# First attention of a two-layer block on one Trainium2 core: running sums by a scan with channels on partitions, in place of triangle products with tokens on partitions

## The chip, the cores and the metric

One core of a Trainium2 chip runs the whole program. The metric is the device time of one execution in microseconds (us); the time of the kernel is the median of ten runs. Engine names are those of the profile: PE is TensorE (matmul), PEld its weight load, DVE is VectorE, ACT is ScalarE, POOL is GpSimd, SP is SyncE, which here only issues transfers.

## The reference, cut to what matters

The input is 16 sequences of 512 tokens with 128 channels. Four stages follow each other, each with a residual and a layernorm: a first attention (below), a mixture of 8 experts that sends every token to one expert, a second attention (softmax, 16 heads of 8 channels, with a bias by distance), and a second mixture with a shared expert. Only the first attention changes. It is a linear attention with 16 heads of 64 value channels; `cexp` is the exponential of a clipped argument:

```python
cross = einsum('bnw,hw->bhn', x, k1) + p1         # p1, p2: sums of sines of the position
diag  = einsum('bnw,hw->bhn', x, k2)
extra = einsum('bnw,hw->bhn', x, k3)
values = einsum('bnw,hwa->bhna', x, value_weight)
cross, diag, extra, p2e = cexp(cross), cexp(diag), cexp(extra), cexp(p2)
num = cumsum(cross * values, axis=2) * p2e * extra + values * diag
den = cumsum(cross, axis=2) * p2e * extra + diag
out = einsum('bhna,hwa->bnw', num / den, output_weight)
```

So for each sequence, head and value channel there is a running sum over 512 tokens, and each token and head has three gates (`cross`, `extra * p2e / den`, `diag / den`) that hold for all 64 channels of the head.

## The kernel before, in words

The 16 sequences go through the four stages in six chunks of 2, 3, 4, 3, 3 and 1. The second attention of a chunk runs together with the first attention and the first mixture of the next chunk and with the second mixture of the chunk itself. Every piece of work is an `op` with an engine, a planned cost, and the buffers that it reads and writes. The order of all ops is written out as a string of two-character ranks (`ORDER`, line 54), and a chain of dependencies without semaphores keeps each engine's instructions in that order. So an instruction that waits holds all that stands behind it on its engine, and SP's transfers too are issued in the order of the list.

Buffers come from pools with fixed counts: `pair` (two PSUM banks, 128 x 1024 f32, three of them), `one` (one PSUM bank, two), `wide` (128 x 1024 f32 in SBUF, twelve), `row` (128 x 512 f32 in SBUF, eleven).

`attention0` makes the gates of one sequence with tokens on partitions: `sc` holds the three scores of each token and head, `ex` their exponentials, `ce` the running sum of `cross` (by products with the triangle `tri` and with ones, L966 and L968), and `den`, `gg` (that is `extra * p2e / den`) and `own` (`diag / (cross * den)`) follow in small VectorE steps (L976 to L990).

`tile0` then does the value part for one sequence and one tile of 128 tokens, four tiles in a row, all 16 x 64 channels side by side in the free dimension:

- PE makes `pv`, the values (L1015, two products of 512 columns); DVE multiplies by `cross` into `ev` (L1028).
- POOL makes `self`, the token's own term, from `ev` and `own` (L1034).
- For tiles 1 to 3 a transfer issued by POOL adds the last row of the tile before (`carry`) to the first row of `ev` (L1041).
- PE makes the running sum `cum` by a product of `ev` with the triangle `tri` (L1050); ACT copies its last rows to `carry` (L1057) for the next tile.
- DVE multiplies `cum` by `gg` into `o` (L1062) and adds `self` (L1066).
- PE turns `o` in eight 128 x 128 transposes into `po` (L1073), ACT copies it to `ot` (L1076), PE multiplies `ot` with the output weights into `y` (L1081), and DVE adds `y` to the tile of `x` (L1089).

So a sequence passes four tiles, each with five `wide` buffers and three `pair` buffers, and each waiting on the carry of the one before.

The rest of the kernel is not touched. Of it, the text names: the second attention's bias add `p<-st,bias` (DVE, L1441) with the exponential (ACT, L1447), its row maxima `low` (bf16, ACT L1333, DVE L1349, L1365 and L1376), its inputs `qk_pad`, which SP loads (L1272, L1285, L1405); and the fetches of expert weights and token rows by indirect transfers that POOL issues (L796).

Of the kernel before, what the change touches and what calls it, by code (L numbers as in the profile page):

```python
# [19 lines left out]
P = 128  # L20
# [34 lines left out]
    "#$###)#9#-#0#.#&#%#(#A#D#'#,#B#G#J#=#7#H#I#K#*#?#L#M#O#F#P#Q#R#W#X#Y#6#C#T#U#Z#<#>#S#a#d#@#3#[#i"  # L55
    "#k#N#4#^#f#m#`#g#l#n#o#t#{#}#/#2#1$-#s#x$4$2$/$c#_#5#r&:#+#:#;%H'Y#u#8#v#w#V#]#b#~$#$$#c#p$'$&$+"
    "$)$*$0$3$:$A#e#z$,$.$7$9$8$<$B$E$K$]$1$6$;$?$D$H$L$M$N$[$a$e$C$G$I$J$T$U$W$Y$b$h$u$y%'%J%Q%R%W%["
    "%l#E#|$F$O$P$S$V$Z$Q$R$f$X$^$`$g$j$k$q%5$_$d$i$m$n$o$v$w$x${%*%@$l$p$r$s$|%,%)%+%-%2%E%M$z%$%(%."
    "%/%6%8%<%A%B%K%N%S%X%Y%^%`%b%c%d%e%f%m&8&Q&q'2&9&?&>&G&H&I&U&Y'.&E&o&R&Z&t&{&}&~'5'$'&'%'3'>'@'P"
    "'['e'#']'T'V'h'n't'u'v(/(2(4(=(@(d(r(s*>+T#y#h#j#q$%$($5$=$t%w$>%1&7%v'A'f(I(G%y'*&i%x$@$}%z'B(>"  # L60
    ")5'?-.(K%t(B(C(S(W(D(O(T(P(N(Y)>)&)d)=(U(x(q(V([)T)e)S)g)<)J)K({(~)$)Q)*)+)-(l(z(})E)1)6)9)C)G)I"
    ")X)m)3):)@)/)2)4)H)r)u*)*;*L)')F(e(k)?)f)c*P*Z*T*U*f*_*w*})O)V)^)Y)Z)j)v*|*`*c*{+'+-+9)W)])i)7)8"
    ")D)x*o*n*t++*u+/+A)N)P)U)(),)0*,*3*z+#+(+>*~+8+K*(***0*#*$*'*5*6*7*S*[+&+N+Q+Y)a)b)R)`+*+5+I+4+G"
    "+H+L+_+P+[+k*:*=*@)s)t)y*A+@+R+X+a+D+W+p*<*B*E)w)z)|*F+E+`+d+s+F+Z+}*C*D*I*4*8*9*J*K+6+g+l+x+;+C"
    ",*)p)~*&*+*/*1*p*q*r*x*y+J,0,4,<*.*-*G*%+h,/,&+n,,+b+f+o,1,8,9*M*Y*^*g*h*i+0+r+w+z,2+v+{,:*]*a*b"
    "*d*e*l+=+i+|,#,@+m+y,C*k*m*s+$+%+.+2+B,%,),5,E,',3,P+1+:+?+)+7+<+O+U+c+t,$,(,X,],`,W,A,F,S,Z,b,m"
    ",N,O,U,d,R,g,w,l,Q,T,[,n,p,~,^,_,i,v,a,j-+-1-5-=-E-[-_-t-u.).8.J.K.u.}.W.r.[.`.x/5/;1H,+,-,e,f,."
    ",7,=,>,D,B,;,M,?,r,H,K,V,L,J-8,s-9-W-/-4-<-2-3-;-O,u,{,}-'-)-0-K-?-A-C,|-#-*-Q-X-&-(-,,h,o,x-R-Y"
    "-Z.$.%.+,I,z,y,q-I---:-V.A.@.I.L.D.Y.c-L-P-`-6-@-B-m.M.S.U.a.O.X.p-d-f-h-J-M-]-p.Q.d.g.s.V.b.~-G"
    "-S-^-e-i-l-n-o.k.h.m.n.t.y/E-a-c-g-s-x-y-z.0.3.B.G.^/F/O/b-U-T-k-H/R.q/V/T/#/I/J/_/'/B/f.,.-.5-v"  # L70
    "-}-~/,/?/K/Q/^/G/H/p.>.E.H./.=.?.j/M/`/g/r/W/d/{.w.z.{.v.|/%/-/./o/h/k/s/v/}/~.e.f.i.6.7.9.l///0"
    "/@/D/j0#0005._.C-{.Z0$0%0+0,/y/w/x0;0)0K0O/$/&/)/*/+/1/<070*0/0J090I0U/(/2/6/[/a/e/i/z030?0Z0.0E"
    "0]/4/8/=/7/>/C/P/U0A0H0P0_0G0Q0b/L/N/]/X/c/q0'0(060=0F0L0q0u0z0W0M0S0T0X0`0k0N0R0V0a0^0h0l0[0i0r"
    "0t0m0o0|0d0n0y1%0v1'1(1)1,1.1415181@1A1C1N1Q1R1^1a1]1b1`1d1g2s3-:{$~%#%%%&%0%4%7%9%3%:%;%?%I%C%D"
    "%F%O%a%i%=%>%L%P%V%_%Z%]%o%{%|&.%T%U%g%h%j&$%n%u&&&'&)&+%p%q%s&%&*&/&2&3&6&=&S'8'F'Z(.(1(8(H%k%r"
    "%G%}%~&#&,&1&;&(&-&A&0&5&<&B&C&F&j&k&4&@&J&K&L&N&V&W&[&c&d&p&D&M&O&P&a&f&g&h&l&r'1'7&`&e&s&w&x&y"
    "&z'+'4':'G'H'L'i'}(#(g(m&X&T&]&^&_&b&u&v&m&n&|'''-'(')'6'9'M'N','/'='D'E'O'J'K'Q'S'a'k';'<'I'R'W"
    "'X'_'`'g'y'z($'U'^'p'q'w'x'|'~()(+(,(-(E(X(f(h(n(u(w(|)%).)[)k*?+~/:/A*R*j*v+,+M+V+e+j-7*Q+q+]+^"
# [12 lines left out]
    "6k6q797%9m9.9l928V8m8o8|8W8d9+7B7M7O767?7@7d8l8t8y9$8x9)9@7]7f7g7I7N7R7k9#8}9'9,909L9d7n7w7z7p7|"
    "8*8.8?8w9?9A9^8~9D9g7U7W7Z7V7Y7[7l8A979O9W9y9p9v9w7J7t7K7<9n9q9o9_:&9z:$:,:':.:K8E8J8M7^7b7i8N:9"
    "9~:#:1:@:C:L9F9K9M9E9J9S9T:-:(:5:6:7:;:M9(93959&9/999;9=:D:):4:=:Q:R:e9V9f9h9Q9R9Y9{:/:<:A:B:N;+"
    ";3;O:U:O:V:i:`:h:~:d:W:b:c:s;#;):r;(;*;1:y;0;@:a;,;2;<:g;5;A;H;K;W;k;l;x;y;{<<<=<D<L<O<Y<s=$<w<|"
    "='=2=HC/:*:0:^:k:8:H:::>:G:S:Y:j:E;n:X:o:]:l:m:x<,:n<%;G;J;Q;%;&;-;];7;>;?;6;;;C;[;P;R;U;V;Z;^;d"
    ";e;.;:;=;j;r;v;};~<#<F<G<H:z:|:p:q;D<Q<P=:<r<b<c=(<v=*=8;S;`;b;X;_;c;w<u=0=5==<z=)=F;z<'</;E;I;M"
    "<2=,=6=;=O=.=Q=r;h;p<$<?<A<K<S<W=1=>=C=P=4=<=z<&<)<3<0<1<5<l<m<q<t<y=7>$>'>.;m;t<+<-=c>>=N=y=n=Z"
    "=_=o=u=}>*<e<j<o<f<h<i=U=G=s=v>(=X=p>E<U<X<[<N<V<a<k={=w=|>:=~>;>H<><B<R<~=%=&=V=W=e>3>8>9=q>1>L"
    "<*<6<7<8<@<E<}=Y=h=t=x><>M>Y>d<^<`=/<]>f>j>l>g>@>A>Q>R>I>W>h=K=S=`=E=J=L>&>B>O>a>v>F>G>}=3=@=A=d"
    "=g=l>)>i>]>`>z>s?#?$=i=j=m=[=b=f>+>C>N>e>r?%>[>b?+>#>0>7>,>->6>K>P>S>Z>c>p?3?4?9>t>y>{?/>w?,?1>x"  # L100
    "?(?*?<>|?5?J?&?.?:?@?-?;?K?)?2?7?I?6?B?L?N?P?R?S?T?U?V?W?X?_?`?a?b?c?j?y?n?s?}@)@bK4'0'C'b'c'd'j"
    "'l'm'o'r's'{(((%('(5(6(9(:(&(*(0(3(<(L(?(A(R(](i)#(7(;(M(Q(a(p(b(c(j(t)h)}(Z(`);)B)L)M)l+S+u-r-|"
    ".'.4.F.N.T.].o5#(J(F(^(_(o)))A)n(v(y){)_)q)o*2*H*O*V*X,c,t->-N.#.&.(.R0&0-0B0j*N*W.1.20Y0f0c0e0s"
    "0}1?1E0:0@0g0w1/11121;1K1V1_1n1p2*2[2n3?3C-j-$040<0p1$1*191&1-1I1M1U1Y1Z1e1t3`3r1>1S1W1X2&2-2+28"
    "494=5W5f2%2)273)5/5=5I5O5h5i6H6I4O4U5B5C5]5m5o5r5v6Q6y7;8)888<8K8Q8T412{4~565[5g5j5w5n5q6@6-6466"
    "6S6T6W757H6V6Y6a6e7P7X7Q7c7j7x828F6[6d7/7e848>8D8Z8^8i8r8z8'838@8P8[8b8h8q8s9%9*9-919B9C9G9H9I9P"
    "9Z9[9]9c:t:u:w9k;8=?:};9;T;a;u<(<9<:<_;o<C<.<4<n<p<x<{>n<I=-=#=+=B=D=R=]>o<J=a=^=k>%>2>4>D>m=M>^"
    ">J>T>_>k>q>u?D>=?'>~?0?8?=?A?F?G?H?Y?]?g?k@-@5@RB'C%@4DRD|GFG{B*DNH~J4KK?d?m?t@.?e?f@L@o?i@p@dAt"
    "A~AuB8B=BKB[BWBfBrC+C-C6BXC5CACVC`D'CbCcD(D<DBHfDxE5F-F0GPGcGSGUGeGvH%K5EiHDGmGyHmI,HuH}I0JgJtKq"
    "FnMGJQJ[MgN%MjMkN*N2N<N@NrO9O>OWOcPNQAP+P,QmVbX4ZVbqR1RKS;UbVAVDYV>X?l?o?~@&?p?z?w?q?u?|@$@A@F@Z"  # L110
    "?{@H@C@@@B@DAr@EA)@c@e@m@_@`@f@{@r@s@xA+A,A0A4@g@h@n@k@q@t@|A&@vA#A$@~A%A'A5A:A<AcAdAv@,@+@>@=@G"
    "A(A2A;AxAwAyB4B#B,B?@;@J@K@S@T@Y@]B3A|B(BCB:BIBR?O@1@3@M@O@P@QB>B2B6BBBFBSBU@'@0@8@9@I@N@y@zBDB;"
    "BABGBQBVB^@7@:@?@U@W@[@aA1A3AQAhA}BaBdBwAIA=AHA/BvBNBeBOBMB+B5BbBPBYBqB%B&B-B)B/B0B7BZBlBmBnB]Bi"
    "ByAzA{B$AXA_AaB.B_BoBpBsBjBkC1AbAfAkA]A`AeB9BHB}B|C&C(C)C2C3AiAjAnApAqAsB1BLBTB`BcBzC7C;CKA-A.@l"
    "@jC#C>B~CSC=C0C:CJC@CICOA6A7A8@u@w@}A9C,C?CDCNC4CLCPAJAKANALAOASAYC.CFCQCgC9CMCxACAFAMA@AAADAUAV"
    "CHCTC_C|CWCzD.APARATABAEAGAZA[A^BEBJC$D@DMDoD-CvC}D#D3D7DGCXCyC~D5CYCiDLDJC{D%D1DPDYD[D0D4D;DID:"
    "DCD_DfDjE%E(E2E9E?EFEMEYEdE{F:FMF;FQF<F?FUG1G6L5C[C]E,E=CaCdCfChCeCjCnCwD]D/CoD6CtD*CsDVDtDgD~D8"
    "D?DDDQDXDaE&DODUDZDTDWDeDvDcDmDnD^DbDlE'E+D=DEDKD>DADSDwE-E.ECEEEPD`D9DHD2EADdF(D{E]E`ElEzE^EfF'"
    "E:E>E@D}E*E/EWF.F+F2F6F3F8FAE1E4E8E$E0E6EJEhF1F=FCEnEsFHEBEHEIE3E7E;E[EpF7FNFSFWF>FaFbEGEKELDkDp"
# [156 lines left out]
def block_kernel(ctx: ExitStack, tc: tile.TileContext, d, out: bass.AP):  # L276
# [16 lines left out]
        "st": (sm, [P, NT, 6], F32, 2),  # L293
        "mv": (sm, [P, NT, 2], F32, 2),
        "rs": (sm, [P, 2, NT], F32, 2),
        "ex": (sm, [P, NT, 3 * H0], F32, 2),
        "gg": (sm, [P, NT, H0], F32, 2),
        "den": (sm, [P, NT, H0], F32, 2),
        "own": (sm, [P, NT, H0], F32, 2),
# [1705 lines left out]
```

## Time and profile before

| | |
|---|---|
| median of ten runs | 2115.08 us (2106.33 to 2119.12) |
| the profiled execution's own time | 2124.05 us |
| its span in the profile | 2122.2 us |
| busy share of the span | PE 92%, DVE 79%, ACT 71%, POOL 38% |
| granted TensorE clock, mean | 0.969 |
| transfers | 240.09 MB, 38% of the 16 DMA engines' time |

The profile is of one execution, which was 0.4% slower than the median. Busy times are sums over instructions of an engine; a group row gives line, engine, operation, output and inputs, shapes and count, then busy time, mean time of one, and the idle time of the engine ahead of the group with what ended it.

### The profile page before, as it was taken

Reading aid. Unit: us, or ns where it says so; the run is one execution under the profiler, and the core shown is the slowest. Engines: PE = TensorE matmul, PEld = TensorE weight load, DVE = VectorE, ACT = ScalarE, POOL = GpSimd, SP = SyncE. Lnnn points to the kernel's source line nnn. Section 1 sums busy time; section 2 is a strip of 40 time slices with the busy share of each in tenths; the row PEclk is TensorE's granted clock in tenths of the full one; section 3 lists DMA queues with packets and bytes.
Section 4 is the critical chain, followed back from the end, with each engine's and each line's share of the span. In section 5 each row is a group of like instructions: output and inputs, shape, how many; then the busy total and the mean of one; then the engine's idle time right before and its main releaser. Section 6 shows DMA issues by size and latency. Waiting matters only on the chain. (4 is left out here: it accounts for less than half of the span.)

```text
span 2122.2 us, 32135 instructions
## 1 busy us (share of the span) xinstructions
PE 1942.0 (92%) x11437; PEld 1040.2 (49%) x11437; DVE 1682.4 (79%) x2894; ACT 1497.7 (71%) x2066; POOL 798.7 (38%) x879
## 2 busy tenths in 40 slices
PE   4888899999999999899999999999999899999888
PEld 1555644444555454345554543456545444543365
DVE  8565579787979778787888697978868798989856
ACT  5222368886877678577779788767687699899753
POOL 5235552325222533631124244533332654131333
PEclk9899999999999999999999999999999999999899
DMA  4514533423332344334024443233154445433353
GB/s 121 137 39 114 152 114 118 148 80 95 116 118 59 99 137 121 107 116 120 23 95 129 138 122 98 88 101 101 51 177 126 142 137 155 144 117 111 95 168 101
DMA packets 188580, 240.09 MB, mean 113 GB/s; under 512 B 22149, under 2 KB 132613, under 8 KB 188421
## 3 DMA queue, kind: packets, MB, share of 16 engines
q1 hardware_dynamic: 162868, 149.36, 23.4%
q0 software_dynamic: 25552, 88.68, 14.1%
q8 instruction: 91, 1.49, 0.3%
q14 instruction: 69, 0.56, 0.1%
HBM read 164.50 MB, written 80.42 MB: 115 GB/s over the span
## 5 line engine op out<-in xcount | busy, mean ns | idle before, releaser
L1441 DVE TENSOR_TENSOR p<-st,bias 128x1024 f32<-128x1024 f32 x512 | 606.7, 1218 | 56.3 <-PE st L1422 47.2
L1333 ACT CAST low<-s 128x1024 bf16<-128x1024 f32 x512 | 499.4, 1019 | 129.4 <-PE s L1317 123.4
L1447 ACT ACTIVATE p<-p 128x1024 f32<-128x1024 f32 x512 | 521.7, 1059 | 77.6 <-DVE p L1441 68.1
L796 POOL DMA_INDIRECT ws<-tab,rows x201 | 204.3, 1016 | 397.8 <-DVE yq L1153 179.1
L1308 PE MATMUL s<-bias,ident 128*128 128x512 bf16 x1024 | 309.2, 397 | 26.6 <-ACT low L1333 14.9
L1456 PE MATMUL av<-p,vaug 128*32 128x512 f32 x2048 | 268.8, 605 | 2.8 <-ACT p L1447 1.5
L1422 PE MATMUL st<-qk_pad 64*128 64x512 f32 x1024 | 228.1, 479 | 31.9 <-DVE p L1441 15.5
L1034 POOL TENSOR_TENSOR self<-ev,own 128x1024 f32<-128x1024 f32 x64 | 125.2, 1958 | 312.8 <-DVE ev L1028 122.2
L1349 DVE TENSOR_TENSOR low<-low 128x1024 bf16<-128x1024 bf16 x256 | 182.7, 721 | 45.7 <-ACT low L1333 42.9
L1422 PEld LDWEIGHTS st<-qk_pad 64*128 64x128 f32 x1024 | 90.6, 185 | 212.1 <-DVE p L1441 82.7
L796 POOL DMA_INDIRECT yg<-results,place x124 | 125.7, 1014 | 121.1 <-issue 52.1
L1308 PEld LDWEIGHTS <-ident 128*128 128x128 bf16 x1024 | 86.3, 99 | 168.5 <-issue 140.4
L1317 PE MATMUL s<-qk_pad 32*128 32x512 bf16 x1024 | 149.4, 389 | 0.2
L1050 PE MATMUL cum<-ev,tri 128*128 128x512 f32 x256 | 130.5, 635 | 15.0 <-DMA ev<-carry 13.1
L1062 DVE TENSOR_TENSOR o<-cum,gg 128x1024 f32<-128x1024 f32 x64 | 78.3, 1223 | 70.8 <-ACT carry L1057 38.6
L1081 PEld LDWEIGHTS y<-ow,ot 128*128 128x128 f32 x1024 | 123.7, 196 | 21.0 <-issue 14.4
L1081 PE MATMUL y<-ow,ot 128*128 128x128 f32 x1024 | 131.1, 283 | 1.4 <-DVE ex L953 0.6
L1015 PE MATMUL pv<-vw,xt 128*128 128x512 f32 x256 | 128.4, 627 | 1.3 <-ACT low L1333 0.5
L626 POOL TENSOR_SCALAR rs<-mv 128x4 f32<-128x4 f32 x63 | 19.8, 315 | 259.0 <-DVE mv L620 254.9
L1028 DVE TENSOR_TENSOR ev<-pv,ex 128x1024 f32<-128x1024 f32 x64 | 77.9, 1220 | 48.1 <-PE pv L1015 47.6
L1076 ACT COPY ot<-po 128x1024 f32<-128x1024 f32 x64 | 64.8, 1013 | 68.0 <-PE po L1073 60.3
L1317 PEld LDWEIGHTS <-qk_pad 32*128 32x128 bf16 x1024 | 35.3, 91 | 149.2 <-issue 142.8
(226 smaller groups left out, 3149.8 us busy)
## 6 DMA issues: line engine op xcount, KB each, us to landing
qk_pad<-parts SPq DMA_DIRECT2D x256, 128.0 KB
parts<-lo SPq DMA_DIRECT2D x32, 512.0 KB
parts<-hi SPq DMA_DIRECT2D x32, 512.0 KB
xq<-tokens SPq DMA_DIRECT2D x42, 256.0 KB
results<-yq SPq DMA_DIRECT2D x42, 256.0 KB
bias<-rows SPq DMA_DIRECT2D x16, 448.0 KB
x<-in_x SPq DMA_DIRECT2D x16, 256.0 KB
xt<-in_xt SPq DMA_DIRECT2D x16, 256.0 KB
```

Of the source, the lines that this page charges most:

```text
L796: nc.gpsimd.indirect_dma_start(out, bass.IndirectOffsetOnAxis(to, 0) if to is not None else None, in_, bass.IndirectOffsetOnAxis(of, 0) if ...
L1015: nc.tensor.matmul(pv()[:, hf, :], xt()[:, col(t)], vw[:, hf * N : (hf + 1) * N], start=True, stop=True,)
L1050: nc.tensor.matmul(cum()[:, hf, :], tri, ev()[:, hf, :], start=True, stop=True)
L1081: nc.tensor.matmul(y()[:, :P], ot()[:, hf, col(c)], ow[:, 4 * hf + c, :], start=(hf == 0 and c == 0), stop=(hf == 1 and c == 3),)
L1308: nc.tensor.matmul(s()[:, i, :], ident16, bias16[:, 4 * g + 2 * jp + i, 2 * u + 1 : 2 * (u + N) : 2], start=True, stop=False,)
L1317: nc.tensor.matmul(s()[:, i, :], pad[r, 0, col(it)], pad[r, 1, :], start=False, stop=True,)
L1333: lambda s=s, jp=jp, low=low: nc.scalar.copy(low().bitcast(BF16).rearrange("p i (j n) -> p (i j) n", j=2)[:, 2 * jp : 2 * jp + 2, :], s(),),
L1349: nc.vector.tensor_tensor(to[:, :, h * (it // 2) : h * (it // 2) + h], v[:, :, :h], v[:, :, h:], ALU.max)
L1422: nc.tensor.matmul(s[jp]()[:, i, :], pad[r, 1, jp, col(jt)], pad[r, 0, jp, :], start=True, stop=True,)
L1441: lambda jp=jp, h=h, pj=pj: nc.vector.tensor_tensor(pj(), s[jp](), bias[:, h : h + 2, u : u + N], ALU.add),
L1447: ACT, 1.0, lambda pj=pj: nc.scalar.activation(pj(), pj(), AF.Exp),
L1456: nc.tensor.matmul(acc()[32 * j : 32 * j + 32, :], va[:, jt, h * VW : h * VW + 32], p[j // 2]()[:, j % 2, :], start=(jt == 0), stop=(jt == ...
```

## The change

The value part of the first attention is laid out the other way: 128 partitions hold two heads of 64 channels, and the 512 tokens lie in the free dimension. A step `s` now handles four heads and all tokens of a sequence (before: all heads and 128 tokens), again four steps per sequence.

- The running sum is one `tensor_tensor_scan` of VectorE over 1024 elements (two heads after each other; the factor is 0 at the first token). Its state is the running sum of `cross` times the values, divided by the token's own `cross`: state = ratio x state + value, with ratio = `cross` of the token before over `cross` of this one.
- The gates (`ratio`, `own` = `diag / den`, `sums` = `gg * cross`) are needed repeated over the 64 channels of a head. They are turned once per sequence (`tp`, four transposes), copied (`rows`), written to a DRAM buffer (`gates0`), and each step reads them back by six transfers of SP, two for each gate, every row repeated over 64 partitions.
- DVE multiplies `own` by the values, POOL makes `sums * ratio` and adds `own`, PE multiplies with the output weights straight from `sums`, and DVE adds `y` to all of `x`.
- Gone are the triangle products of the values (`cum`), the carry with its copy and its transfer, the eight transposes of `o` and the copy `ot`.
- `ORDER` is another string: all ops have been ranked anew.

```diff
-        "ex": (sm, [P, NT, 3 * H0], F32, 2),
+        "ex": (sm, [P, NT, 4 * H0], F32, 2),
...
+    gates0 = [dp.tile([4 * H0, N], F32, tag=f"gates{i}", name=f"gates{i}") for i in range(2)]
...
         def early():
             nc.vector.tensor_tensor(gg(), p2e, part(2), ALU.mult)
-            nc.vector.reciprocal(own(), part(0))
-            nc.vector.tensor_tensor(own(), own(), part(1), ALU.mult)
+            nc.vector.reciprocal(part(2), part(0))
...
             nc.vector.reciprocal(den(), den())
+            nc.vector.tensor_tensor(part(1), part(1), den(), ALU.mult)
             nc.vector.tensor_tensor(gg(), gg(), den(), ALU.mult)
-            nc.vector.tensor_tensor(own(), own(), den(), ALU.mult)
+            nc.vector.tensor_tensor(part(3), gg(), part(0), ALU.mult)
...
+        def turn():
+            for t in range(NT):
+                nc.tensor.transpose(tp()[: 4 * H0, col(t)], ex()[:, t, :], ident)
...
+            ACT, 0.5, lambda: nc.scalar.copy(rows()[: 4 * H0], tp()[: 4 * H0]), reads=[tp],
...
+        def ratios():
+            to = rows()[4 * H0 : 5 * H0]
+            nc.vector.memset(to[:, 0:1], 0.0)
+            nc.vector.tensor_tensor(
+                to[:, 1:], tp()[2 * H0 : 3 * H0, 1:], rows()[:H0, : N - 1], ALU.mult
+            )
...
+        for f, first, n, key in ((0, 4 * H0, H0, (rows, 1)), (1, H0, 3 * H0, rows)):
...
+                lambda f=f, first=first, n=n: nc.sync.dma_start(
+                    gates0[b % 2][f * H0 : f * H0 + n], rows()[first : first + n]
+                ),
...
+    def heads0(b, s, x, xt):
+        pv, y = buf("pair", f"pv_{n}"), buf("one", f"y0_{n}")
+        ratio, own, sums = (buf("wide", f"{k}_{n}") for k in ("ratio", "own", "sums"))
+        for f, to in ((0, ratio), (1, own), (3, sums)):
+            def spread0(f=f, to=to):
+                for i in range(2):
+                    src = gates0[b % 2][f * H0 + 4 * s + 2 * i : f * H0 + 4 * s + 2 * i + 2]
+                    nc.sync.dma_start(
+                        to()[:, i, :], src.unsqueeze(1).to_broadcast([2, A0, N])
+                    )
...
         def values():
-            for hf in range(2):
+            for i in range(2):
                 nc.tensor.matmul(
-                    pv()[:, hf, :], xt()[:, col(t)], vw[:, hf * N : (hf + 1) * N],
+                    pv()[:, i, :], vw[:, (2 * s + i) * P : (2 * s + i + 1) * P], xt(),
                     start=True, stop=True,
                 )
...
-            lambda: nc.vector.tensor_tensor(split(ev), split(pv), heads(ex(), t), ALU.mult),
...
-            lambda: nc.gpsimd.tensor_tensor(split(self_), split(ev), heads(own(), t), ALU.mult),
...
-                lambda: nc.gpsimd.dma_start(
-                    ev()[0:1].rearrange("p f n -> p (f n)"),
-                    carry()[P - 1 : P].rearrange("p f n -> p (f n)"), accum_op=ALU.add,
-                ),
...
-                nc.tensor.matmul(cum()[:, hf, :], tri, ev()[:, hf, :], start=True, stop=True)
...
-            lambda: nc.vector.tensor_tensor(split(o), split(cum), heads(gg(), t), ALU.mult),
...
-            DVE, 1.3, lambda: nc.vector.tensor_tensor(o(), o(), self_(), ALU.add),
...
-                    nc.tensor.transpose(po()[:, hf, col(c)], o()[:, hf, col(c)], ident)
...
-        op(ACT, 1.0, lambda: nc.scalar.copy(ot(), po()), reads=[po], writes=[ot])
...
+            lambda: nc.vector.tensor_tensor_scan(
+                flat(ratio), flat(ratio), flat(pv), 0.0, ALU.mult, ALU.add
+            ),
...
+            DVE, 1.15, lambda: nc.vector.tensor_tensor(own(), own(), pv(), ALU.mult),
...
+            POOL, 2.0, lambda: nc.gpsimd.tensor_tensor(sums(), sums(), ratio(), ALU.mult),
...
+            POOL, 2.0, lambda: nc.gpsimd.tensor_tensor(sums(), sums(), own(), ALU.add),
...
         def product():
-            for hf in range(2):
-                for c in range(4):
+            for t in range(NT):
+                for i in range(2):
                     nc.tensor.matmul(
-                        y()[:, :P], ot()[:, hf, col(c)], ow[:, 4 * hf + c, :],
-                        start=(hf == 0 and c == 0), stop=(hf == 1 and c == 3),
+                        y()[:, col(t)], sums()[:, i, col(t)], ow[:, 2 * s + i, :],
+                        start=(i == 0), stop=(i == 1),
                     )
...
+            DVE, 0.6, lambda: nc.vector.tensor_tensor(x(), x(), y(), ALU.add),
```

## The prediction

> **What bounds the kernel now.** I read the page's busy shares first, then the busy time by stage.
>
> ```profile
> span 2122.2 us, 32135 instructions
> PE 1942.0 (92%) x11437; PEld 1040.2 (49%) x11437; DVE 1682.4 (79%) x2894; ACT 1497.7 (71%) x2066; POOL 798.7 (38%) x879
> ```
>
> The stages are cut where the work changes: 42 is where the first values start, 280 where the second attention starts, 1645 where the first attention's last `y` is added. Columns: stretch, length, busy time (and count) of PE, PEld, DVE, ACT, POOL, then granted clock, DMA share, GB/s.
>
> ```profile
> 0.00:42.00 42.00, 14.26 (x32) 3.24 (x32) 33.53 (x31) 23.19 (x25) 26.73 (x46) 0.93 0.46 126
> 42.00:280.00 238.00, 202.84 (x1002) 133.95 (x1001) 133.32 (x261) 73.28 (x118) 99.08 (x93) 0.90 0.39 108
> 280.00:1645.00 1365.00, 1292.18 (x7777) 679.30 (x7776) 1127.82 (x1890) 1037.17 (x1421) 488.48 (x514) 0.98 0.36 108
> 1645.00:2000.00 355.00, 330.24 (x2004) 154.72 (x2003) 309.79 (x564) 307.40 (x416) 141.15 (x165) 0.98 0.41 124
> 2000.00:2122.00 122.00, 102.53 (x629) 68.96 (x628) 77.98 (x152) 56.69 (x89) 43.30 (x63) 0.96 0.47 147
> ```
>
> PE is the densest engine in both stages that hold the first attention: 85% of 42:280 (B) and 95% of 280:1645 (C), where DVE has 83%. What comes after 1645 (477 us) holds none of it. So the change can act on B and C alone: 22 of the 64 tiles lie in B, 42 in C.
>
> **What goes, by tile.** The rows, one of each per tile (PE's products are several records):
>
> ```profile
> L1050 PE MATMUL cum<-ev,tri 128*128 128x512 f32 x256 | 130.5, 635 | 15.0 <-DMA ev<-carry 13.1 <-ACT h L1143 1.0 <-DVE p L1441 0.3
> L1073 PE MATMUL po<-ident,o 128*128 128x128 f32 x512 | 70.4, 282 | 15.4 <-DVE o L1066 13.3 <-DVE den L985 0.5 <-DVE p L1441 0.4
> L1028 DVE TENSOR_TENSOR ev<-pv,ex 128x1024 f32<-128x1024 f32 x64 | 77.9, 1220 | 48.1 <-PE pv L1015 47.6
> L1062 DVE TENSOR_TENSOR o<-cum,gg 128x1024 f32<-128x1024 f32 x64 | 78.3, 1223 | 70.8 <-ACT carry L1057 38.6 <-PE cum L1050 30.5 <-PE av L1456 1.6
> L1066 DVE TENSOR_TENSOR o<-o,self 128x1024 f32<-128x1024 f32 x64 | 84.3, 1317 | 5.5 <-POOL self L1034 2.4
> L1034 POOL TENSOR_TENSOR self<-ev,own 128x1024 f32<-128x1024 f32 x64 | 125.2, 1958 | 312.8 <-DVE ev L1028 122.2 <-PE av L1456 51.5 <-DVE own L990 28.9
> ```
>
> PE loses 130.5/64 = 2.04 us (`cum`) and 70.4/64 = 1.10 us (`po`) a tile. It gains four transposes per sequence, half of the eight of a `po`, 0.55 us, 16 times. PE: -130.5 - 70.4 + 8.8 = -192 us. The value and output products (L1015, L1081) keep number and shape. ACT loses `ot` (64.8) and `carry` (48.3) and gains 16 copies of 128x512 at 0.59: -104 us. POOL loses `self` (125.2) and the carry's issues (43.2) and gains two products of that shape per step, 2 x 64 x 1.958 = 250.6: +82 us, to 881, or 44% of the time forecast.
>
> **What comes, on DVE.** The scan is not there in this size, but small ones are:
>
> ```profile
> L744 DVE TENSOR_TENSOR_SCAN upto<-fresh,cnt 128x96 f32<-128x96 f32 x6 | 2.1, 358 | 0.2
> L754 DVE TENSOR_TENSOR_SCAN end<-ones,size 128x8 f32<-128x8 f32 x11 | 1.9, 175 | 0.4
> ```
>
> 88 more elements take 183 ns, 2.08 ns each; 1024 elements take 0.358 + 928 x 0.00208 = 2.29 us. The lower bound is 1.22 us, the elementwise row of the same size; I take 2.29, since scans gave the slope. `own` times `pv` is a row like L1028, 1.22. The add of `y` is now 128x512, as in L1524, 0.686, in place of 0.281. A step: 2.29 + 1.22 + 0.69 = 4.20 us. A tile had (77.9 + 78.3 + 84.3 + 17.9)/64 = 4.04. Per sequence `ratios` adds about 0.69 (128x512, at most) and a memset of 0.1.
>
> One more term is a wait between DVE and POOL. Its rows (min/median/max, ns):
>
> ```profile
> L1349 DVE TENSOR_TENSOR low<-low x256: 628/685/2940, 298.1 to 2003.8; 128x1024 bf16<-128x1024 bf16 x128
> L1441 DVE TENSOR_TENSOR p<-st,bias x512: 1160/1218/1226, 323.4 to 2032.3; 128x1024 f32<-128x1024 f32 x171
> ```
>
> The maxima, with both inputs in SBUF, stretch to 2.9 us, and every one that does lies on a POOL product; the bias add, with one input in PSUM, never does. Means over medians give what it costs now: (721 - 685) x 256 = 9 us for L1349, (743 - 691) x 128 = 7 for L1365, 2 for L1376, together 18 us. Twice the POOL time doubles it: +18 us, all in C. The scan and `own` read PSUM, so I give them none. New between scan and `y` are POOL's two products, 3.9 us, in a queue that also holds the weight fetches (L796), whose single waits reach 27 us; PE's output product waits for them in order, and with it the second attention's products behind it. Before, the add of `self` waited 2.4 us in all on POOL. I take nothing; one full wait of 27 us in each of the six chunks, 160 us, is the far end, and belongs to the slower cases.
>
> The Trainium skill, page "SBUF — State Buffer", section "Who interferes with whom", speaks against the change here: a VectorE operation with two SBUF inputs and a GpSimd operation that reads SBUF exclude each other, and the second waits until the first ends. Taken by itself, with POOL's 250 us over some 2000 and half an operation's wait, 512 maxima would lose about 512 x 0.125 x 0.98 = 63 us (an estimate from that rule); the trace shows the waits but fewer, and the sum goes by the trace.
>
> **Transfers.** 64 x 6 + 32 = 416 more issues on SP at 0.42 to 0.67 us (its timeline, 256 KB loads), about 190 us more on a queue that mostly waits (its longest wait is 278 us for `mx`, L1405). Their 384 x 256 KB = 101 MB, at the rate of SP's queue,
>
> ```profile
> q1 hardware_dynamic: 162868, 149.36, 23.4%
> ```
>
> are 15.8% more, from 38% to 54% of the DMA engines: no bound. Repeating one row is no dearer: the load of `lin`, one row to 128 partitions, was issued at 1.26 us and used at 4.65. The spreads are ranked ahead of the scans, so I cost them at nothing where work is dense. A sequence's first scan needs turn 0.55, copy 0.59, `ratios` 0.7, the way to DRAM (`rounds` issued at 279.42, its readers from 282.02: 2.6) and back (3.4): 7.8 us. Later sequences' lie under the work of others; the first one's is open.
>
> **The sum.** C: PE 1292 - 81.3 - 44.9 + 6 = 1172. DVE by the tiles' busy time in this stretch: 1128 - 49.9 - 51.3 - 51.2 - 11.8 (42 adds) + 42 x 4.20 + 11 x 0.79 + 18 = 1167. PE's clock may fall with its share (0.95 in 800:900, where PE had 88%): 1172 x 0.98/0.95 = 1209, no term. The two are level, so the end is set by how dense DVE can run: 88 to 91% in the densest 100 us windows (1700:1800 88.4, 1800:1900 88.6, 500:600 90.7, 1900:2000 91.5). I take 89.5%: 1167/0.895 = 1304, -61 us (PE then 90%). B: PE 202.8 - 49.2 - 25.4 + 3 = 131, DVE about 136. There a chain runs, and PE's share was 65% in 0:100 and 81% in 100:200; at the middle, 73%, 131 us make 180, and the first gates' 8 us make 188: -50 us. Together -111: the profiled execution's 2124 becomes 2013. It stood 9 us over the median, so 2115 becomes **2004 us**.
>
> **The rivals.** *DVE is full earlier.* In 1645:2000 DVE had only 87.3% beside PE's 93%. At that share C is 1167/0.873 = 1337, -28; B gives half, -25: 2062 us. For it: DVE gets no lighter, and a 2.3 us scan stands ahead of the bias adds that ACT waits for (68 us of ACT's wait is on them). The skill's page "Perfetto Trace Analysis", section "Identifying the Most-Contended Engine", goes further: matmul busy time is no measure of PE's headroom; its arithmetic rate and the weight-load share are. By that page (PEld 49%, DVE 79%) C would give nothing and B alone 2065.
>
> *All of PE's time is had.* C keeps its ratio of span to the fullest engine, 1365/1292 = 1.056: 1167 x 1.056 = 1233, -132; B gives its 72: 1911 us. Against it: two engines would have to be 95% full at once.
>
> *SP holds DVE: slower.* The six spreads of a step wait for free `wide` buffers, and behind them on SP stand `qk_pad` loads of the second attention; the built order also lets each transfer wait for the one eight before it. A late spread stops the scan and all DVE work behind it. From 111/64 = 1.7 us of such a stop a step the gain is gone; one landing (3.4 us) a step makes +218 - 111: about 2220 us, half of that 2113. For it: issues on SP nearly double. Against it: of some 1600 us that SP waited, these landings took about 170 (tokens 84, `parts` 61, `rounds` 21), and the order has most scans far behind their spreads.
>
> That the products stay is excluded: the built order holds no `cum` and no `po`.
>
> **How the numbers follow.** Forecast 0.42, DVE full 0.22, all of PE's time 0.08: faster 0.72. SP holds DVE: slower 0.25, and 0.03 between; 0.2% (4 us) is about what this kernel's measurement can tell. The range runs from 1935, midway between the all-PE case and the forecast with the scan at its lower bound (42 x 1.07/0.895 = 50 less, 1954), to 2150, which is two thirds of a landing a step (2004 + 146); the faster cases alone lie at 1935 to 2070. About 0.05 is left out below and 0.13 above.
>
> **What would show it.** Right: PE near 1750 us, DVE near 1710, scans near 2.29 us, `y` done for the last time well before 1645, second attention from about 230. Wrong: scans over 2.6 us; DVE waits at the scan on `ratio` transfers of over 60 us in sum; SP's wait for landings grown to hundreds of us; the stage after the last `y` changed in length.

## Result and profile after

| | before | after |
|---|---|---|
| median | 2114.26 us (46 runs, 2103.02 to 2121.33) | 3631.31 us (13 runs, 3622.64 to 3640.54) |
| ratio, with its 95% interval | 1 | 1.718 (1.7159 to 1.7202) |
| the profiled execution's span | 2122.2 us | 3628.5 us |
| granted TensorE clock, mean | 0.969 | 0.754 |

The changed kernel is slower by 1517 us. 2004 us was forecast, so not even the sign held. From the page of the changed kernel, its span, its busy shares and SP's queue:

```profile
span 3628.5 us, 31400 instructions
PE 2007.7 (55%) x10733; PEld 1062.1 (29%) x10733; DVE 1740.8 (48%) x2862; ACT 1394.7 (38%) x1968; POOL 920.0 (25%) x895
q1 hardware_dynamic: 214324, 252.13, 21.2%
```

DVE, ACT and POOL were busy about as long as forecast (DVE 1741 us for 1710, POOL 920 for 881), but no engine is busy for even 60% of the span, and SP's queue takes a smaller share of the 16 DMA engines than before (21.2% for 23.4%). Something holds everybody. The waits say what (engine, line, waited for: us in total, times, longest):

```profile
POOL sums L1076 <- DMA sums<-gates: 908.2, 34, 58.9
DVE ratio L1066 <- DMA ratio<-gates: 507.9, 35, 41.6
ACT low L1335 <- PE s L1319: 505.4, 143, 39.3
PEld y L1087 <- POOL sums L1080: 480.3, 22, 57.7
PE y L1087 <- POOL sums L1080: 467.4, 21, 56.9
ACT ex L959 <- DVE ex L407: 439.9, 14, 155.3
DVE own L1072 <- DMA own<-gates: 407.2, 38, 34.0
```

The first, second and last rows wait for the spreads, the transfers that bring a gate back from DRAM with each row repeated over 64 partitions. DVE stands 915 us for `ratio` and `own`, POOL 908 us for `sums`, and PE's 467 us on POOL are read here as the same wait passed on. By the stages of the prediction (columns as there; 42 us is where the first values start, 933 where the second attention starts, 3148 where the last `y` is added):

```profile
42.00:933.00 891.00, 198.61 (x782) 144.42 (x783) 148.96 (x261) 38.59 (x89) 141.44 (x96) 0.58 0.21 69
933.00:3148.00 2215.00, 1358.47 (x7284) 688.78 (x7283) 1166.44 (x1860) 970.52 (x1352) 565.00 (x527) 0.77 0.30 97
3148.00:3628.50 480.50, 430.40 (x2632) 223.50 (x2630) 391.34 (x715) 362.43 (x504) 186.24 (x227) 0.98 0.42 128
```

These three were 238, 1365 and 477 us before. All of the loss lies where spreads run. What comes after the last `y` kept its length (480 for 477 us), as the prediction said of that stage.

How long is one spread? SP's instructions that issue them (min/median/max in ns), and two of them on its timeline (start, length, in us):

```profile
L1041 SPq DMA_DIRECT2D ratio<-gates x128: 490/3536/11230, 60.5 to 3040.1; - x128
L1041 SPq DMA_DIRECT2D sums<-gates x128: 482/3956/10266, 61.8 to 3069.5; - x128
L1041 SPq DMA_DIRECT2D own<-gates x128: 482/4642/9543, 70.9 to 3035.6; - x128
```

```profile
65.68 5.14 SPq L1041 DMA_DIRECT2D sums<-gates  x1
70.92 5.17 SPq L1041 DMA_DIRECT2D own<-gates  x1
```

The prediction priced an issue at 0.42 to 0.67 us. Here these two block SP for 5.1 and 5.2 us, and the next one follows at once. Over the whole kernel the issues of the 384 spreads last 1301 us in sum, 3.4 us each. Of the stretch around these two the windows view gives

```profile
64.00:85.00 21.00, 0.00 (x0) 0.00 (x0) 2.98 (x2) 0.00 (x0) 0.00 (x0) 0.50 0.13 49
```

PE does nothing, and the DMA share is 0.13. Two engines of sixteen, always busy, are 0.125. The packet records agree: between 63 and 85 us two packets are in flight for 91% of the time and three for the rest, and from 60 to 3145 us it is two or three for 64% of the time. The records name no engine; if two engines share a spread of 256 KB, each moves 64 of its packets of 2 KB, at some 84 ns each 5.4 us with no overlap.

The spread's source is two rows of `gates0`, each repeated 64 times: as an access pattern [2, 64 with step 0, 512]. e1_interleaved, e2_one_head and e3_two_outer_distinct_rows below show that its outermost size of 2 is the cause.

### The profile page after: what moved, and what is told of

Same layout as the page of the kernel before. It is cut to its first block, busy times and chain, and to the rows that moved or that the text cites. A ratio compares the mean times of both kernels' runs of the same rounds, so it can differ in the third digit from the quotient of the medians.

```text
span 3628.5 us, 31400 instructions
## 1 busy us (share of the span) xinstructions
PE 2007.7 (55%) x10733; PEld 1062.1 (29%) x10733; DVE 1740.8 (48%) x2862; ACT 1394.7 (38%) x1968; POOL 920.0 (25%) x895
## 3 DMA queue, kind: packets, MB, share of 16 engines
q1 hardware_dynamic: 214324, 252.13, 21.2%
## 5 line engine op out<-in xcount | busy, mean ns | idle before, releaser
L1443 DVE TENSOR_TENSOR p<-st,bias 128x1024 f32<-128x1024 f32 x512 | 606.6, 1217 | 269.6 <-PE st L1424 209.3
L1076 POOL TENSOR_TENSOR sums<-sums,ratio 128x1024 f32<-128x1024 f32 x64 | 150.7, 2356 | 1466.7 <-DMA sums<-gates 908.2
L1310 PE MATMUL s<-bias,ident 128*128 128x512 bf16 x1024 | 334.8, 423 | 228.0 <-DVE own L1072 100.5
L1087 PE MATMUL y<-ow,sums 128*128 128x128 f32 x1024 | 186.6, 357 | 470.4 <-POOL sums L1080 467.4
L1066 DVE TENSOR_TENSOR_SCAN ratio<-ratio,pv 128x1024 f32<-128x1024 f32 x64 | 146.0, 2283 | 545.3 <-DMA ratio<-gates 507.9
L1087 PEld LDWEIGHTS y<-ow,sums 128*128 128x128 f32 x1024 | 173.8, 264 | 497.0 <-POOL sums L1080 480.3
L1072 DVE TENSOR_TENSOR own<-own,pv 128x1024 f32<-128x1024 f32 x64 | 77.7, 1217 | 433.9 <-DMA own<-gates 407.2
L1319 PE MATMUL s<-qk_pad 32*128 32x512 bf16 x1024 | 174.0, 416 | 164.8 <-DMA qk_pad<-rounds 164.6
L1080 POOL TENSOR_TENSOR sums<-sums,own 128x1024 f32<-128x1024 f32 x64 | 151.9, 2375 | 172.3 <-DVE own L1072 103.7
L636 ACT ACTIVATE x<-x,rs 128x128 f32<-128x128 f32 x192 | 79.1, 487 | 217.0 <-POOL rs L629 211.3
L1051 PE MATMUL pv<-xt,vw 128*128 128x512 f32 x256 | 150.4, 720 | 17.0 <-DMA vw<-in_vw 8.2
```

Of the source, the lines that this page charges most:

```text
L1076: POOL, 2.0, lambda: nc.gpsimd.tensor_tensor(sums(), sums(), ratio(), ALU.mult),
L1080: POOL, 2.0, lambda: nc.gpsimd.tensor_tensor(sums(), sums(), own(), ALU.add),
L1087: nc.tensor.matmul(y()[:, col(t)], sums()[:, i, col(t)], ow[:, 2 * s + i, :], start=(i == 0), stop=(i == 1),)
L1310: nc.tensor.matmul(s()[:, i, :], ident16, bias16[:, 4 * g + 2 * jp + i, 2 * u + 1 : 2 * (u + N) : 2], start=True, stop=False,)
L1319: nc.tensor.matmul(s()[:, i, :], pad[r, 0, col(it)], pad[r, 1, :], start=False, stop=True,)
L1443: lambda jp=jp, h=h, pj=pj: nc.vector.tensor_tensor(pj(), s[jp](), bias[:, h : h + 2, u : u + N], ALU.add),
```

## Experiments

The experiments ran in three series. The kernel before ran in each of them, and its median was 2146, 2142 and 2112 us; every ratio below is to the kernel before of the same series. A point is a hundredth of that time. Between series, ratios may differ by somewhat more than their intervals say. Each expectation is quoted as it stood before its run.

**First series: what makes a spread slow?** Theory A: the transfer is confined to as many DMA engines as its outermost size. Theory B: one row read 64 times is slow in itself.

*e1_interleaved.* The repeats go outermost; partition p then holds channel p/2 of head p%2, and the host lays out the value and output weights to match.

```diff
-                        to()[:, i, :], src.unsqueeze(1).to_broadcast([2, A0, N])
+                        to()[:, i, :], src.unsqueeze(0).to_broadcast([A0, 2, N])
```

> The spreads read a gate row with the 64 repeats outermost and the two heads inside (partition = 2 x channel + head; the value and output weights are laid out to match), all else as in the changed kernel. Theory A (a transfer whose outermost dimension is 2 runs on 2 of the 16 DMA engines, so each spread takes 5.2 us and SP's issue waits for it): the 384 spreads shrink to under 1.5 us each, SP's issue of one back to about 0.45 us, DVE's wait on ratio transfers from 508 us to under 60; time 1980 to 2090 us. Theory B (one DRAM row read 64 times over is slow in itself): spreads stay at about 5 us and the time within 5% of 3631 us.

Measured: 2218.46 us, ratio 1.0331 (1.0299 to 1.0362). Same bytes, same count of transfers, same repeats: only the order of two dimensions differs (and with it which channel lies on which partition), and 68 of the 72 points of loss are gone. DVE's wait for `ratio` transfers is down to 10.4 us, and the issue of a spread to medians of 562 to 588 ns:

```profile
L1041 SPq DMA_DIRECT2D ratio<-gates x128: 312/566/1266, 60.1 to 1636.7; - x128
```

In 64 to 85 us 16 packets or more are in flight for 83% of the time, where it was two in the changed kernel. The time that theory A gave, 1980 to 2090 us, was missed all the same: with quick spreads the kernel is still slower than before.

*e2_one_head.* One transfer for each head, 64 repeats outermost, twelve a step in place of six.

```diff
-                    src = gates0[b % 2][f * H0 + 4 * s + 2 * i : f * H0 + 4 * s + 2 * i + 2]
-                    nc.sync.dma_start(
-                        to()[:, i, :], src.unsqueeze(1).to_broadcast([2, A0, N])
-                    )
+                    for h in range(2):
+                        src = gates0[b % 2][f * H0 + 4 * s + 2 * i + h]
+                        nc.sync.dma_start(
+                            to()[A0 * h : A0 * h + A0, i, :], src.partition_broadcast(A0)
+                        )
```

> Twelve spreads a step, one head each (64 repeats outermost), the layout of the changed kernel kept. Theory A: each runs on all 16 engines, under 1 us of data; SP issues 768 in place of 384, some 190 us more on SP than with the interleaved layout; time 2000 to 2150 us. Theory B: still 64 reads of one row in a row: about 3600 us.

Measured: 2293.39 us, ratio 1.0683 (1.0641 to 1.0726). Here the partitions stay as they were and the number of transfers doubles, and most of the loss is gone again, though not down to theory A's 2000 to 2150 us. It is 75 us slower than e1_interleaved, with 384 issues more (median 594 ns, 228 us of SP): the count of issues matters, but some twenty times less than the shape.

*e3_two_outer_distinct_rows.* The shape of the change, outermost 2, but 128 different rows of `x` in place of two repeated ones; the gates are not read, so the values are others.

```diff
-                    src = gates0[b % 2][f * H0 + 4 * s + 2 * i : f * H0 + 4 * s + 2 * i + 2]
...
-                        to()[:, i, :], src.unsqueeze(1).to_broadcast([2, A0, N])
+                    src = rows_of[130 * i : 130 * i + 130].rearrange("(h a) n -> h a n", h=2)
+                    nc.sync.dma_start(to()[:, i, :], src[:, :A0, :])
```

> The spreads keep their outermost dimension of 2 and their size, but read 128 different rows (of the input x, so the result is not the attention's; the gates are still written to DRAM but not read). Theory A: no change, 3500 to 3700 us, spreads of about 5 us each. Theory B: 2000 to 2200 us.

Measured: 3673.6 us, ratio 1.7113 (1.7048 to 1.7178). No row is repeated, and the whole loss is there: issues have medians of 3.96 to 4.63 us, and in 64 to 85 us two packets are in flight for 92% of the time. Theory B falls. That an outermost size of 2 makes the spread slow is shown; that it means two engines is read from the packets in flight and the DMA share.

*e4_one_spread_a_gate.* Both heads' pairs in one 512 KB transfer per gate and step, 64 repeats outermost (192 spreads in all), weights laid out to match.

```diff
-                for i in range(2):
-                    src = gates0[b % 2][f * H0 + 4 * s + 2 * i : f * H0 + 4 * s + 2 * i + 2]
-                    nc.sync.dma_start(
-                        to()[:, i, :], src.unsqueeze(1).to_broadcast([2, A0, N])
-                    )
+                src = gates0[b % 2][f * H0 + 4 * s : f * H0 + 4 * s + 4]
+                nc.sync.dma_start(
+                    to().rearrange("p i n -> p (i n)"),
+                    src.rearrange("(h i) n -> h (i n)", i=2).unsqueeze(0).to_broadcast([A0, 2, 2 * N]),
+                )
```

> As the interleaved layout, with the heads paired so that one transfer of 512 KB brings a gate of a step (192 spreads, rows of 4 KB). Theory A: as the interleaved one or up to 30 us faster by 192 fewer issues on SP (about 90 us of SP time): 1960 to 2090 us. Theory B: about 3600 us.

Measured: 2205.04 us, ratio 1.0252 (1.0218 to 1.0285): the fastest kernel here that computes the reference with the new layout, and still slower than before and than the 1960 to 2090 us of theory A. A spread in it, and the same stretch as above, from its lines and windows:

```profile
L1040 SPq DMA_DIRECT2D ratio<-gates x64: 447/538/2464, 60.1 to 1632.5; - x64
```

```profile
64.00:85.00 21.00, 10.80 (x59) 8.79 (x60) 14.16 (x20) 0.36 (x1) 9.36 (x4) 0.72 0.80 308
```

0.54 us for twice the bytes, a DMA share of 0.80 for 0.13, and 308 GB/s for 49.

So one mistake explains 69 of 72 points. But with it mended, the prediction of 0.948 times before is still missed by nearly 8 points. From the page of e4_one_spread_a_gate, and the groups that differ from the forecast's terms (busy us, mean ns):

```profile
span 2219.8 us, 30914 instructions
PE 1865.3 (84%) x10627; PEld 986.2 (44%) x10733; DVE 1775.4 (80%) x2862; ACT 1394.4 (63%) x1968; POOL 928.8 (42%) x895
q1 hardware_dynamic: 192052, 252.14, 36.9%
```

```profile
L1351 DVE TENSOR_TENSOR low<-low 128x1024 bf16<-128x1024 bf16 x256 | 204.2, 806 | 61.2 <-ACT low L1335 56.5 <-issue 1.7
...
L1080 POOL TENSOR_TENSOR sums<-sums,own 128x1024 f32<-128x1024 f32 x64 | 155.4, 2430 | 13.0 <-DVE gates L1013 5.5 <-issue 3.2 <-DVE own L1072 0.2
L1087 PE MATMUL y<-ow,sums 128*128 128x128 f32 x1024 | 153.5, 312 | 64.8 <-POOL sums L1080 52.7 <-DMA xt<-in_xt 9.4 <-issue 1.9
L1076 POOL TENSOR_TENSOR sums<-sums,ratio 128x1024 f32<-128x1024 f32 x64 | 152.7, 2386 | 287.6 <-DVE ratio L1066 184.9 <-DMA sums<-gates 55.3 <-ACT low L1335 18.5
L1066 DVE TENSOR_TENSOR_SCAN ratio<-ratio,pv 128x1024 f32<-128x1024 f32 x64 | 145.7, 2278 | 30.2 <-PE pv L1051 15.5 <-issue 7.2 <-PE lg_l L1735 6.3
```

The scan is on its forecast (2278 ns for 2.29 us). POOL's products are not (2.39 and 2.43 us for 1.958), the row maxima are stretched more (806 ns for 721 before), and PE waits 52.7 us for POOL at `y`, where the prediction took nothing. The next two series start from this kernel and ask which of these the time follows.

**Second series: one engine at a time.**

*f1_values_twice.* The product of the values is done twice, 113 us more of PE.

```diff
+                for _ in range(2):
                     nc.tensor.matmul(
```

> The version with one 512 KB spread a gate (2205 us, 1.025 of before), and PE makes the values of each step twice (the same result; four more 512-column product pairs of records, some 1.8 us of PE a step, 115 us in all). Theory C (the removed PE time came back as half clock: PE idles more, its granted clock fell from 0.97 to 0.915): the filler keeps the clock up, 0.93 to 0.96, and the time rises by at most 25 us, ratio 1.015 to 1.035. Theory P (PE's own order is what the span follows): 60 to 115 us more, ratio 1.05 to 1.08.

Measured: 2271.01 us, ratio 1.0612 (1.0582 to 1.0642), 3.6 points or 77 us above e4_one_spread_a_gate. Two thirds of what PE is given still comes out as time, though PE is busy for only 84% of the span. The granted clock did rise, from 0.915 to 0.930, as theory C had it, but the time rose as theory P had it.

*f2_add_on_dve.* POOL's addition of `own` is moved to DVE.

```diff
-            POOL, 2.0, lambda: nc.gpsimd.tensor_tensor(sums(), sums(), own(), ALU.add),
+            DVE, 1.3, lambda: nc.vector.tensor_tensor(sums(), sums(), own(), ALU.add),
```

> The same version with the second POOL product, the add of own to sums, on DVE instead (same place in the list; the result is the same). POOL loses 155 us, DVE gains 64 x 1.22 = 78 us less some 25 us of maxima that no longer wait for POOL. Theory L (POOL's two products, 2.4 us each and with the lock against DVE's two-SBUF maxima, cost the time): 15 to 50 us faster, ratio 1.00 to 1.018. Theory D (DVE is the engine that the span follows): 30 to 60 us slower, ratio 1.04 to 1.055.

Measured: 2232.61 us, ratio 1.0439 (1.0406 to 1.0473), 1.9 points slower. This is in the range of theory D. DVE is the dearer place, although its busy time rose by only 31 us, since the first group of row maxima fell back from 806 to 740 ns.

*f3_add_on_an_eighth.* POOL adds `own` to 128 of the 1024 elements only; the rest of the own term is left out.

```diff
-            POOL, 2.0, lambda: nc.gpsimd.tensor_tensor(sums(), sums(), own(), ALU.add),
+            POOL, 2.0, lambda: nc.gpsimd.tensor_tensor(sums()[:, :, :64], sums()[:, :, :64], own()[:, :, :64], ALU.add),
```

> The same version with the POOL add on 128 of 1024 elements only (the rest of the own term is left out, so the result is not the attention's). Theory L: 30 to 80 us faster, ratio 0.99 to 1.01, PE's wait for POOL at y and the stretched maxima both about halved. Theories C, P and D: within 15 us, ratio 1.018 to 1.030.

Measured: 2155.44 us, ratio 1.0081 (1.0048 to 1.0114). This is in the range of theory L: 121 us less of POOL give 1.7 points, some 37 us, though POOL is busy for only 42%. Of theory L's two signs neither came in full: PE's wait for POOL at `y` fell from 52.7 to 38.9 us and the first group of maxima from 806 to 778 ns, not by half. DVE's busy time fell by 38 us too (1775 to 1738), so whether the gain came by PE's wait or by DVE's shorter work isn't separated.

*f4_product_for_scan.* A plain product stands in for the scan (1213 ns for 2278); the running sum is left out.

```diff
-            lambda: nc.vector.tensor_tensor_scan(
-                flat(ratio), flat(ratio), flat(pv), 0.0, ALU.mult, ALU.add
-            ),
+            lambda: nc.vector.tensor_tensor(ratio(), ratio(), pv(), ALU.mult),
```

> The same version with a plain product of ratio and pv in place of the scan (1.22 for 2.28 us; the running sum is left out, so the result is not the attention's). DVE loses 68 us. Theory D: 45 to 70 us faster, ratio 0.992 to 1.005. Theories C, L and P: under 20 us, ratio 1.015 to 1.027.

Measured: 2169.99 us, ratio 1.0153 (1.0116 to 1.019). 68 us less of DVE give 1.0 point, 21 us: less than theory D had, and at the edge of the other theories' ranges. No one engine is the bound by itself.

**Third series: two reliefs together (a relief takes work off one engine), and the bytes.**

*g1_product_and_eighth.* The edits of f3_add_on_an_eighth and f4_product_for_scan together, leaving out what they leave out.

> The two reliefs in one kernel: POOL's add on an eighth of its elements and a plain product for the scan (the running sum and most of the own term are left out), with one spread a gate on all engines. Alone they took 1.7 and 1.0 points off the 1.025 of the kernel with one spread a gate. Theory A (each engine's work is a delay of its own, and they add): 0.993 to 1.003. Theory O (both shorten the same chain spread, scan, POOL, y, so the second adds little): 1.004 to 1.010.

Measured: 2085.96 us, ratio 0.9867 (0.9843 to 0.9891). Both theories missed: the two give 3.8 points together where they gave 2.7 one by one. Against g4_small_spreads_first_two, which ran in the same series with nearly all of e4_one_spread_a_gate's work, it is 3.8 points too, so that the second adds little is excluded; why they give more than their sum is open.

*g2_small_spreads.* A spread moves 16 pieces of 32 bytes, and the scan, `own` and POOL's product read the weight tile `vw` in its place. All engine work and all issues stay, 101 MB go, and the values are others.

```diff
-                    to().rearrange("p i n -> p (i n)"),
-                    src.rearrange("(h i) n -> h (i n)", i=2).unsqueeze(0).to_broadcast([A0, 2, 2 * N]),
+                nc.sync.dma_start(to()[:16, 0, :8], src[:1, :8].to_broadcast([16, 8]))
...
-                flat(ratio), flat(ratio), flat(pv), 0.0, ALU.mult, ALU.add
+                flat(ratio), vw, flat(pv), 0.0, ALU.mult, ALU.add
```

> The spreads are cut to 16 rows of 32 bytes; the scan, own and POOL's product read a constant weight tile of the same size in their place, so all engine work and the count of issues stay, and the 101 MB go. Theory T (transfers: in 42 to 280 us the DMA engines were 64 to 85% busy and PE only 57 to 64%, so the first chunk waits for bytes): 1.025 falls to 0.985 to 1.000. Theory E (engines and their order alone; the transfers are hidden, as forecast): 1.018 to 1.027.

Measured: 2154.29 us, ratio 1.0193 (1.0166 to 1.0221). With the repeats outermost the bytes cost half a point or so. Theory T falls, E holds.

*g3_small_spreads_and_reliefs.* The edits of g1_product_and_eighth and g2_small_spreads together.

> Small spreads, the plain product and POOL's add on an eighth together: PE's lighter load with next to nothing of what the change adds. Theory T: 0.955 to 0.980, since all three reliefs add. Theory E: as without small spreads, 0.993 to 1.010. If it stays over 0.99, PE's own order and lower clock hold the time, and the forecast of 0.948 failed on PE first.

Measured: 2056.76 us, ratio 0.9717 (0.9689 to 0.9745), in T's range, though T had fallen in g2_small_spreads. In the same series it is 98 us below g2_small_spreads, where the two reliefs alone had given 37 and 21, and 29 us below g1_product_and_eighth. Taking the bytes away gives 29 us beside lighter engines and 11 us beside full ones (g4_small_spreads_first_two less g2_small_spreads); the likely reading is that the bytes were hidden behind POOL and DVE and no longer are when these are lighter.

*g4_small_spreads_first_two.* Small spreads for the first chunk's two sequences only (the edit of g2_small_spreads, for `b < 2`).

> Small spreads only for the two sequences of the first chunk, full ones for the other fourteen. If the bytes hurt in the first chunk, where nothing else is there to cover them: at least two thirds of what small spreads everywhere gain. If they hurt everywhere through contention: about an eighth of it, 1.02 to 1.025. Theory E: 1.022 to 1.027.

Measured: 2165.69 us, ratio 1.0243 (1.0216 to 1.0271), which can't be told from e4_one_spread_a_gate's 1.0252, and the first row maximum on DVE comes at the same place (315.8 us for 315.4). While the engines have all of their work, the first chunk waits for them and not for bytes, although the DMA engines were 74% busy in 42 to 298 us of e4_one_spread_a_gate.

## Why the prediction was wrong, point by point

**Transfers: the step that failed.** The price of a spread was wrong, in the time of SP and in the time of the transfer. It was taken from two rows that do not fit the spread. For the issue it used 256 KB loads of SP's timeline, and for the repeat it said "Repeating one row is no dearer" and named the load of `lin`. But `lin` goes to 128 partitions as one outermost dimension; the spread's is 2. What was looked at was the repeat, which e3_two_outer_distinct_rows shows to cost nothing, and not the order of dimensions, which e1_interleaved shows to cost 68 points. The average over 16 engines then hid it: the text worked out that the spreads were 15.8% more "of the DMA engines: no bound". In engine time that is 0.158 x 16 x 2122.2 = 5365 us; on two engines it is 2682 us, longer than the kernel. The runs show 0.212 x 16 x 3628.5 - 0.235 x 16 x 2152.6 = 4214 us (the queue's time after, less that of g2_small_spreads), 2107 us for each of two engines. And where 190 us more were forecast on SP, the sum of SP's issue instructions rose from 418 to 2271 us: 1301 of the spreads, and 970 of all else that SP issues, which had been the 418.

A row that fits stood in the trace of the kernel before. `rows<-line` (L592) is a transfer of SP that repeats rows too, 23 times each, with 4 rows as its outermost dimension, from DRAM to DRAM. The first one ran alone:

```profile
65.99 0.72 SPq L592 DMA_DIRECT2D rows<-line  x1
72.21 0.67 SPq L602 DMA_DIRECT2D bias<-rows  x1
```

Its 92 packets of 4 KB, 377 KB, took from 67.5 to 71.9 us, 86 GB/s, with four packets in flight for most of the time (65%), where e4_one_spread_a_gate moved 308 GB/s in 64 to 85 us. The next transfer, which reads what it writes, was issued at 72.21 us. So two, four and 16 or more packets in flight go with outermost sizes of 2, 4 and 64. The same timeline had issues that hold SP far longer than 0.67 us, for a reason that isn't shown (two took 12.21 us):

```profile
80.61 12.21 SPq L671 DMA_DIRECT2D tokens<-zero  x2
```

This is the place where the prediction should have drawn on a rule. The Trainium skill, page "DMA: Bandwidth & Descriptors", states under "Why a DMA increments its semaphore by 16 and not by 1" that the engine count is the largest number up to 16 that divides the slowest dimension (of size over 1) of both access patterns. Under "Rules for kernel authors" the same page says that an outermost dimension smaller than 16 confines the whole transfer to at most so many engines. The DMA share of 0.13 in 64 to 85 us and the two packets in flight agree with it for a size of 2. With 64 repeats as the outermost size, the share is 0.80.

**The rival "SP holds DVE".** It was right in kind: the spreads stop the scan and all DVE work behind it, and the sign to look for, DVE waits on `ratio` transfers of over 60 us, stands at 507.9 us. Its price was wrong: one landing (a transfer's time until it has arrived) of 3.4 us a step. A step issues six spreads one after the other, and at the 5.2 us of the stretch above that is 6 x 5.2 = 31 us, an estimate. It reasoned from how long one landing takes and not from how many spreads two engines can serve. That is also why the range did not hold the time. One sign misled: SP's wait for landings grew only from 194 to 252 us and not by hundreds, because the time is within SP's issue instructions.

**The rest, with the spreads on sixteen engines.** g2_small_spreads has all of the change's engine work and almost none of its bytes, and ran beside a kernel before of 2112 us, so that its stages can be set against the forecast's. Its boundaries are put as in the prediction: B ends 18 us before the first row maximum on DVE, C with the last `y`. First g2_small_spreads, then g3_small_spreads_and_reliefs:

```profile
42.00:290.00 248.00, 156.69 (x785) 115.15 (x785) 151.28 (x260) 38.07 (x88) 143.39 (x97) 0.81 0.33 95
290.00:1671.00 1381.00, 1244.61 (x7282) 631.61 (x7283) 1196.11 (x1862) 968.97 (x1353) 578.49 (x527) 0.94 0.37 110
1671.00:2152.60 481.60, 433.27 (x2628) 224.63 (x2627) 390.65 (x715) 361.91 (x504) 185.90 (x227) 0.97 0.42 128
```

```profile
42.00:250.00 208.00, 148.92 (x774) 109.35 (x774) 116.12 (x254) 36.56 (x85) 100.29 (x96) 0.82 0.41 108
250.00:1574.00 1324.00, 1217.11 (x7299) 621.01 (x7300) 1123.82 (x1868) 968.68 (x1359) 498.46 (x527) 0.97 0.38 115
```

| us | before | forecast | small spreads | and with reliefs |
|---|---|---|---|---|
| B | 238 | 188 | 248 | 208 |
| C | 1365 | 1304 | 1381 | 1324 |
| after the last `y` | 477 | 477 | 482 | 481 |

- *B.* "I take nothing" for POOL's two products between scan and `y` was a term that failed. In e4_one_spread_a_gate PE waited 52.0 us for `sums` within 42 to 330 us, in 16 waits, and POOL had 143 of B's 248 us to work in g2_small_spreads (99 of 238 before). With the reliefs B shrinks by 40 us. POOL's product isn't all of it: beside e4_one_spread_a_gate, the first row maximum comes 18 us earlier in f3_add_on_an_eighth and 13 us earlier in f4_product_for_scan, and with the reliefs B is 21 us longer where the bytes are moved (229 us in g1_product_and_eighth). Before, POOL's `self` lay beside the running sum; now its products lie between the scan and PE, and nothing else is there yet to cover them.
- *POOL's rate.* Both products were costed at 1.958 us, the row of `self`; they took 2.39 and 2.43, 58 us more in all. The row's second input was a gate read over 64 columns again and again, while the new ones read two full tiles; whether that is the reason wasn't tried.
- *Row maxima.* "Twice the POOL time doubles it" gave 36 us of stretch; (806 - 683) x 256 + (825 - 691) x 128 + (748 - 683) x 64 ns = 53 us came in e4_one_spread_a_gate, three times before's 18: POOL's products took 308 us for `self`'s 125, 2.5 times and not twice. The 63 us that the prediction set aside for the trace's count were nearer.
- *C.* DVE had 1196 us of work for 1167 and ran at 86.6% for 89.5%. 1196/0.895 = 1336 would be the time by the work alone; the other 45 us are density. The rival "DVE is full earlier" had 87.3%, and 1196/0.873 = 1370 is close to the 1381 measured, so it had DVE's density nearly right. But it too forecast a faster kernel (2062 us), and that DVE sets this density isn't shown: f1_values_twice, f3_add_on_an_eighth and f4_product_for_scan each move the time. The other reading on record, by which C gives nothing, was nearer still for C (1381 us for 1365), but it had B bring a gain.
- *PE's clock.* "No term" was wrong. PE lost its 192 us of work (x11437 instructions to x10733), but its busy time fell only from 1942 to 1854 us, for 1750 forecast. The granted clock went from 0.90 to 0.81 in B and from 0.98 to 0.94 in C, and 131 x 0.90/0.81 + 1172 x 0.98/0.94 = 1367 us is most of the way from the forecast's 1303 to the 1401 measured in B and C. PE with gaps was granted a slower clock, and by this sum 64 of the 192 us went back that way. What this cost in time isn't shown: f1_values_twice raised the clock and the time with it.

**What stays open.** How much of the 8 points each of these terms holds isn't settled. With POOL's second product cut to an eighth, the scan's extra time gone and the bytes gone, 0.972 is left, not 0.948. PE's 1217 us in C of that kernel are 45 above the forecast's at nearly the forecast's clock (0.97). That the written order, planned for a POOL product of 2.0 us and a spread at 1.1 us of SP, is a part of this wasn't tried. No version was found that computes the reference and beats the kernel before.

## What to carry to other kernels

Before a transfer is priced, write down its access pattern from the outside in: the row that it is compared with must have the same outermost size, not only the same bytes and repeats. A DMA share is an average over sixteen engines, so a share of 13% may be two engines that are full; look for the waits on its transfers and for long issue instructions instead. And an engine that is 40% busy still costs time when the work given to it is put between two dense engines: price the new chain first, then the shares.

## What the runs showed of the hardware

- A slow transfer shows in the issuing engine. With an outermost size of 2, SP's issue instruction itself lasted 3.5 to 4.6 us (medians) and 11.2 at most, against 0.54 us with 64 (median, e4_one_spread_a_gate); so whoever reads only the waits of SP finds little.
- Packets in flight followed the outermost size: two at 2 (the changed kernel), four at 4 (`rows<-line` before), 16 or more for 83% of the time at 64 (e1_interleaved, 64 to 85 us).
- An issue with 64 repeats outermost took nearly the same for 256 KB (562 to 588 ns, e1_interleaved) as for 512 KB (534 to 542, e4_one_spread_a_gate).
- The scan of 1024 f32 took 2278 ns and a product of the same size 1213. The slope of two scans of 8 and 96 elements had predicted the scan's 2.29 us.
- In 64 to 85 us of the changed kernel, where PE did nothing, the granted clock was 0.50; over its whole span, with PE busy for 55%, it was 0.754, with 84% 0.915 (e4_one_spread_a_gate) and with 92% 0.969 (before).
